# Last queries' stage of a decoder layer: attended chunks, reciprocals, stores and operand loads at other places, residual tiles in other buffers

## The chip, the cores and the metric

One Trainium2 chip, one of its NeuronCores. The metric is device time in microseconds (us) of one execution of the whole program; the time before is 2362.86 us, the median of 3 runs (2362.38 to 2368.84). Engines are called as the profile calls them: PE (TensorE matmul), PEld (its weight loads), DVE (VectorE), ACT (ScalarE), POOL (GpSimd), SP (SyncE, which here only issues DMAs).

## The reference

A pre-norm decoder layer on x of (2, 2048, 512), that is 4096 tokens, and a context of (2, 154, 512). In short:

```python
x = x + linear_attention(layernorm(x))        # 16 heads of 32, 128 features
x = x + cross_attention(layernorm(x), context)
x = x + experts(layernorm(x))                 # 8 experts, 6 picked, and a shared one
# linear_attention:
q_proj, k_proj = elu1(q @ proj), elu1(k @ proj)      # per head
kv, k_sum = k_proj^T v, sum(k_proj)                  # over all tokens of a batch
z = 1 / (q_proj . k_sum + 1e-8)
out = (q_proj kv * z) @ w_out + b_out
```

The layernorms have no weights. kv and k_sum are sums over all the keys of a batch, so no query of a batch can be finished before all its keys are done.

## The kernel before, in words

Tokens are cut into 8 blocks of 512 (`nblk`), 4 blocks to a batch (`bpb`); 512 columns are 4 chunks of 128 (`NC`), and a block is 4 tiles of 128 tokens (`NT`). Each fp32 matmul of a product is made of three fp32r matmuls on high and low parts (`TERMS`), so a 128x512 output of `product` takes 12 matmuls. One function writes the whole program, stage after stage:

1. Keys, values and queries of all blocks; on the way the queries of the first batch (blocks 0 to 3). Their numerators go to DRAM (`numd`). This ends near 493 us.
2. **The last queries' stage**, which the change touches: the queries of blocks 4 to 7, 16 chunks, one a step (`steps`, `for n in range(len(steps) + 1)`), from about 493 to 672 us. Beside them the attention output of blocks 0 to 5 is finished, and cross attention is begun.
3. Cross attention, with the attention output of blocks 6 and 7 at its start; then the experts.

What a step n of stage 2 does. `load_queries` (line 294 for its DMAs) loads the operand `qst` of a chunk, three DMAs of 256 KB. `query_features` makes four heads' features: a matmul `pqp` (L474), two activations (L359, L360) and a DVE instruction (L361, `e_q`). `numerators` and `denominators` of the chunk of the step before are 16 matmuls `pn` and `pd` (L230), then a copy `num` (L500). They are pinned: `tc.keep_in_program_order` ties each to the PE instruction written before it. After a block's fourth chunk `reciprocals` (L520) sends `den` to DRAM (`dd`, L523), reads it back spread out (`z`, L529), takes a DVE reciprocal (L532), pinned in the same way, and stores it (`zd`, L533).

Beside that runs the output of older blocks. `load_reciprocals` reads `zd` as `zr` (L546), `attended` multiplies `num` by it on POOL (L558), copies to a high part `at` on ACT (L559) and subtracts for a low part on DVE (L118). `load_numerators` brings `numd` of a block back by a DMA of 1 MB issued on POOL (L541). `attention_out` calls `out_tile` for each of a block's four tiles: load the residual tile `xr_a` (L306), add the bias row on POOL (L307), 12 matmuls `po_a` (L148), add on DVE (L310), store to `x1` (L311). `out_tile` also makes the output tiles of cross attention (`cross_out`).

What sets the order. Work that should fill gaps is a generator in `dense.waiting`; `dense.fill(k)` runs k of its matmuls at that place of the program, and `dense.after(k, f)` calls f when k such ticks have gone by. Program order is then only a priority: the context has `schedule_with_timeline_sim=True`, and when the program is built each engine's queue is put in the order in which the instructions are expected to become ready. On the chip each queue runs in that order and waits at its head. A tile's tag has a number of buffers, handed out in program order: a tile gets its buffer when its first writer goes, and a later tile of the tag does not go ahead of it. The tags that matter here:

- `b8` (17 buffers of 8 KB a partition): `qst`, the pairs `at`, `num` of a block, weights such as `xwq`, the layernorm's outputs, the cross attention's operands `xst`;
- `xs` (5 buffers): residual tiles `xr_a`, layernorm tiles `xsx`, raw weight tiles `xswout`, `xsxwq`;
- `hl` (4 buffers): the `zr` pairs, the high and low parts of queries on their way to DRAM;
- `eq` (5 buffers of the pool `early`): features of the first batch's queries. This pool is closed ahead of stage 2, and the pool `res`, with the four key tiles `xkst` of cross attention (`load_keys`, 12 DMAs issued on POOL, L631), takes its place in memory.

In the loop of stage 2, at the start of step n, `load_queries` is called for step n+1 and `attended` for two chunks (the table `ahead`: n to block and first chunk); in an even step the four output tiles of that block are added to `dense` and the next `load_numerators` follows. Then the four heads' features are written, in two halves with a `dense.fill` of 13 (later 14) after each, and after the second half the pinned numerators and denominators.

Of the kernel before, what the change touches and what calls it, by code (L numbers as in the profile page):

```python
# [9 lines left out]
F32 = mybir.dt.float32  # L10
# [7 lines left out]
P = 128  # L18
D = 512
# [5 lines left out]
NT = TB // P  # L25
# [12 lines left out]
def decoder_layer(  # L38
# [26 lines left out]
    nc = tc.nc  # L65
    tokens = x.shape[0]
    nblk = tokens // TB
    bpb = nblk // batches
# [4 lines left out]
    work = ctx.enter_context(tc.tile_pool(name="work", bufs=4))  # L73
# [8 lines left out]
    attending = ctx.enter_context(ExitStack())  # L82
    early = attending.enter_context(tc.tile_pool(name="early", bufs=5))
# [11 lines left out]
    def bank(name):  # L95
        return ps.tile([P, 512], F32, tag="ps", name=name)

    def eight(shape, dtype, name):
        return big.tile(shape, dtype, tag="b8", name=name)

    def half(name, dtype=F32):
        return work.tile([P, 512], dtype, tag="kp", name=name, bufs=9)
# [4 lines left out]
    def tile_of(d, b, t):  # L107
        at = b * TB + t * P
        return d[at : at + P, :]

    def load_row(d, name):
        row = rowp.tile([P, D], F32, tag="row", name=name)
        nc.sync.dma_start(out=row, in_=d.to_broadcast([P, D]))
        return row

    def low(dst, src, hi, eng=None):

        (eng or nc.vector).tensor_tensor(dst, src, hi.bitcast(F32), ALU.subtract)  # L118
# [7 lines left out]
    def split_weight(raw, name, busy=False):  # L126

        hi = eight([P, NC, D], FR, f"{name}_hi")
        lo = eight([P, NC, D], FR, f"{name}_lo")
        for k in range(NC):  # L130
            if isinstance(raw, list):
                part = raw[k]
            else:
                part = load_tile(raw, 0, k, name)
            if busy:
                nc.gpsimd.tensor_scalar(hi[:, k], part, 1.0, None, ALU.mult)
            else:
                nc.scalar.copy(hi[:, k], part)
            low(lo[:, k], part, hi[:, k], nc.gpsimd if busy or k % 2 else nc.vector)
        return hi, lo  # L140
# [3 lines left out]
    def product(dst, pairs):  # L144

        todo = [(a[i], b[j]) for a, b in pairs for i, j in TERMS]
        for n, (a, b) in enumerate(todo):
            nc.tensor.matmul(dst, lhsT=a, rhs=b, start=n == 0, stop=n == len(todo) - 1)  # L148
            yield
# [68 lines left out]
    dense = Dense()  # L218
# [16 lines left out]
    def fl(k, f):  # L235
        return int((k + 1) * f + 1e-6) - int(k * f + 1e-6)
# [55 lines left out]
    def stack(dst, d, parts=(0, 1, 0)):  # L292
        for r, part in enumerate(parts):
            nc.sync.dma_start(
                out=dst[r * HD : (r + 1) * HD].bitcast(F32),
                in_=d[part].rearrange("(h d) n -> d h n", d=HD),
            )
# [1 line left out]
    def store_pair(d, hl):  # L299
        nc.sync.dma_start(out=d.rearrange("r p n -> p r n"), in_=hl.bitcast(F32))  # L300

    def out_tile(name, src, dst, row, parts, w):


        xs = work.tile([P, D], F32, tag="xs", name=f"xr_{name}", bufs=5)
        nc.sync.dma_start(out=xs, in_=src)  # L306
        nc.gpsimd.tensor_tensor(xs, xs, row, ALU.add)  # L307
        po = bank(f"po_{name}")
        yield from product(po, [(part, (w[0][:, c, :], w[1][:, c, :])) for c, part in enumerate(parts)])
        nc.vector.tensor_tensor(xs, xs, po, ALU.add)  # L310
        nc.sync.dma_start(out=dst, in_=xs)  # L311

    x1 = [dram.tile([TB, D], F32, name=f"x1_{b}") for b in range(nblk)]
    x2 = [dram.tile([TB, D], F32, name=f"x2_{b}") for b in range(nblk)]
# [4 lines left out]
    xs = [half(f"xs{t}") for t in range(NT)]  # L319
# [8 lines left out]
    for t in range(NT):  # L328
# [4 lines left out]
        a = nc.scalar.copy(hi, pt)  # L333
        b = nc.vector.tensor_tensor(lo, pt, hi.bitcast(F32), ALU.subtract)
# [132 lines left out]
    def load_queries(b, c):  # L467
        qsts[b, c] = eight([3 * HD, 4, TB], FR, f"qst{b}_{c}")
        stack(qsts[b, c], qd[b][c])
# [47 lines left out]
    def reciprocals(b, pd):  # L517

        den = half(f"den{b}")
        nc.vector.tensor_scalar(den, pd, Z_EPS, None, ALU.add)  # L520
        dd = dram.tile([4, NC, TB], F32, name=f"dd{b}")
        for h in range(4):
            nc.sync.dma_start(out=dd[h], in_=den[h * HD : h * HD + NC, :])  # L523
        z = small.tile([P, H * TB // P], F32, tag="z", name=f"z{b}", bufs=1)
        flat = "h c n -> (h c n)"
        zd = dram.tile([4, NC, TB], F32, name=f"zd{b}")

        def turned():
            nc.sync.dma_start(out=z, in_=dd.rearrange(flat).rearrange("(p n) -> p n", p=P))  # L529

        def stored():
            tc.keep_in_program_order(nc.vector.reciprocal(z, z))  # L532
            nc.sync.dma_start(out=zd.rearrange(flat).rearrange("(p n) -> p n", p=P), in_=z)  # L533

        dense.after(10, turned)
        dense.after(18 if b < nblk - 1 else 24, stored)
        zds[b] = zd

    def load_numerators(b):
        nums[b] = eight([P, NC, TB], F32, f"num{b}")  # L540
        nc.gpsimd.dma_start(out=nums[b], in_=numd[b])  # L541

    def load_reciprocals(b, c):
        two = pair_of(f"zr{b}_{c}").bitcast(F32)
        for h in range(4):
            nc.sync.dma_start(  # L546
                out=two[h * HD : (h + 1) * HD],
                in_=zds[b][h : h + 1, c : c + 2].to_broadcast([HD, 2, TB]),
            )
        for i in range(2):  # L550
            zrs[b, c + i] = two[:, i]

    def attended(b, c):

        if c == 0:
            ats[b] = [eight([P, NC, TB], FR, f"at{b}_{i}") for i in range(2)]
        at = nums[b][:, c]
        nc.gpsimd.tensor_tensor(at, at, zrs.pop((b, c)), ALU.mult)  # L558
        nc.scalar.copy(ats[b][0][:, c], at)  # L559
        low(ats[b][1][:, c], at, ats[b][0][:, c])  # L560

    def attention_out(b, t):
        if not 0 <= b < nblk:
            return
        rows = slice(t * P, (t + 1) * P)
        hi, lo = ats[b]
        parts = [(hi[:, c, rows], lo[:, c, rows]) for c in range(NC)]
        yield from out_tile(f"a{b}_{t}", tile_of(x, b, t), tile_of(x1[b], 0, t), bout, parts, wout)


    scale = 1.0 / math.sqrt(HD)
# [187 lines left out]
    for s in range(ws_gate.shape[1] // F):  # L759
# [9 lines left out]
        out=before,  # L769
        in_=before,  # L770
# [498 lines left out]
    for n in range(nblk * per):  # L1269
        b, c, t = n // per, n // NT % NC, n % NT  # L1270
# [12 lines left out]
        if (b, c, t) == (nblk - 1, 3, 0):  # L1283
            load_numerators(0)
            load_reciprocals(0, 0)
            bout = load_row(b_out, "bout")
# [10 lines left out]
    for m in range((nblk - bpb) * per - shift, (nblk - bpb) * per + NT):  # L1297
# [3 lines left out]
            sums_step(m)  # L1301
        if m % 4 == 1:
            load_queries(*chunks[bpb * NC])
    attending.close()
    res = attending.enter_context(tc.tile_pool(name="res", bufs=1))


    wout = split_weight(w_out, "wout")
    steps = chunks[bpb * NC :]

    ahead = {n if n < 13 else n + 2: ((n - 1) // 2, (n - 1) % 2 * 2) for n in range(1, 15)}
    for n in range(len(steps) + 1):
        if n < len(steps):
            b, c = steps[n]
            if n + 1 < len(steps):
                load_queries(*steps[n + 1])
        for i in range(2):
            if n in ahead:
                attended(ahead[n][0], ahead[n][1] + i)
        if n + 1 in ahead:  # L1320
            load_reciprocals(*ahead[n + 1])
        if n in ahead and ahead[n][1]:
            whole = ahead[n][0]
            if whole < nblk - 2:
                dense.add(*(attention_out(whole, t) for t in range(NT)))
            if whole + 1 < bpb:
                load_numerators(whole + 1)
        if n == 7:
            ln, tr = layernorm(x1[0], 0, 0, qts, "x")
            dense.add(*ln[:3])  # L1330
            ln = ln[3:]
        if n == 8:
            dense.add(*tr[:1], *ln, *tr[1:])
        if n == 11:
            dense.add(*(cross_query(0, i) for i in range(NC)))
        for i in range(2):
            if n < len(steps):
                query_features(b, c, 2 * i)
                query_features(b, c, 2 * i + 1)
            dense.fill(fl(2 * n + i, 13 if n < 12 else 14))  # L1340
            if n and i:
                columns.batch()
                numerators(*steps[n - 1])
                denominators(*steps[n - 1])
        if n == 10:
            xwq = split_weight(wq_t, "xwq")
        if n == 11:
            for i in range(NC):
                load_keys(0, i)
    summed_up.close()  # L1350
# [2 lines left out]
    steps = [(b, c, t) for b in range(nblk) for c in range(NC) for t in range(NT)]  # L1353
    for n in range(len(steps) + LAG + 1):
        if n < len(steps):
            b, c, t = steps[n]
# [44 lines left out]
        if n > LAG:  # L1401
            b, c, t = steps[n - LAG - 1]
# [47 lines left out]
    for n, (group, u) in enumerate(todo3):  # L1450
# [3 lines left out]
        ahead = [[], []]  # L1454
        if u == len(units) - 2 and more:
            ahead = [expert_ahead(b) for b in range(group[-1] + 1, group[-1] + 3)]
        parts = products(n) if n else ready
# [123 lines left out]
```

## Time and profile before

| what | us |
|---|---|
| median of 3 runs | 2362.86 (2362.38 to 2368.84) |
| the profiled execution | 2363.39 |
| its span, first to last instruction | 2361.7 |
| PE busy | 2243.7 (95%) |
| DVE, POOL, ACT busy | 1670.7 (71%), 1218.7 (52%), 1105.2 (47%) |
| PE busy in 504 to 580, 76 us | 66.03, clock 0.94, DMA 234 GB/s |
| PE busy in 580 to 663, 83 us | 67.71, clock 0.90, DMA 215 GB/s |
| PE busy in 663 to 676, 13 us | 5.43, clock 0.67, DMA 164 GB/s |

The page's second part cuts the span into 40 slices of 59 us; a digit is the busy share in tenths, and PEclk is the clock that TensorE was granted. In a list by time, a row is start, length, engine, line, operation, output<-input and count; in brackets stands how long the engine was idle before it and what it waited for. In the list of waits, a row is who waited for whom, us in total, times, and the longest.

### The profile page before, as it was taken

The page shows a single profiled execution, that of the slowest core. Times are in us where ns is not written, and L with a number is a line of the kernel's source. Part 1 is how long each engine was busy: PE and PEld are TensorE (multiplying, and loading weights), DVE is VectorE, ACT ScalarE, POOL GpSimd, SP SyncE. Part 2 cuts the span into 40 slices and gives each one's busy share as a digit, 9 for nine tenths or more (in the row PEclk, how much of TensorE's full clock was granted, in tenths as well). Part 3 has the DMA queues.
Part 4 walks back from the last instruction along what each step waited for, and adds up shares of the span by engine and source line. Part 5 has one row for each costly group of instructions (what it writes and reads, how often), then busy time and mean ns, then how long its engine had stood idle before and what let it go on. Part 6 is the DMA issues. An engine that isn't in the chain of part 4 may idle for free.

```text
span 2361.7 us, 35144 instructions
## 1 busy us (share of the span) xinstructions
PE 2243.7 (95%) x11978; PEld 1735.2 (73%) x11978; DVE 1670.7 (71%) x2777; ACT 1105.2 (47%) x2598; POOL 1218.7 (52%) x1086
## 2 busy tenths in 40 slices
PE   7999999897878999998999999999999999999999
PEld 5888777654556777776778877888778888788887
DVE  6555564666567777778877786677887778977777
ACT  4555676754556667776433343322333222432221
POOL 5545333645356565554655553545555455754543
PEclk9999999998989999999999999999999999999999
DMA  6655777997765566564766654655547555575553
GB/s 207 181 171 169 208 214 218 253 254 214 224 189 174 159 188 171 169 193 174 263 240 240 227 192 186 243 199 227 193 170 277 205 205 218 210 260 198 223 187 129
DMA packets 194896, 485.63 MB, mean 206 GB/s; under 512 B 26970, under 2 KB 46810, under 8 KB 174782
## 3 DMA queue, kind: packets, MB, share of 16 engines
q1 hardware_dynamic: 192990, 477.30, 61.3%
q0 software_dynamic: 1728, 6.09, 0.9%
q8 instruction: 95, 1.56, 0.3%
q14 instruction: 83, 0.68, 0.1%
HBM read 345.01 MB, written 138.31 MB: 205 GB/s over the span
## 4 chain that ended last, share of the span: by engine, by line
PE 51%; DMA 7%; DVE 7%; POOL 3%; issue 2%; ACT 1%; SPq 0%; DVEq 0%; ACTq 0%; POOLq 0%
PE pg L1045 26%; PE pf L1158 10%; PE pf L148 3%; PE po_x L148 3%; PE xpq L148 2%; PE pc L737 2%; PE xpt L717 1%; PE psc L685 1%; DMA xr_x<-x 1%; DMA wq<-wqs 1%; DMA xqd<-xhl 1%; DMA xsx<-x 1%; DMA xst<-xqd 1%; DMA x<-xr_x 1%; DVE nb L692 1%
## 5 line engine op out<-in xcount | busy, mean ns | idle before, releaser
L1045 PE MATMUL pg<-xo,wq 128*128 128x512 f32 x3360 | 826.1, 394 | 8.5 <-DMA wq<-wqs 3.5
L1045 PEld LDWEIGHTS pg<-xo,wq 128*128 128x128 f32 x3360 | 631.6, 189 | 151.0 <-ACT s L1056 5.8
L1179 DVE TENSOR_TENSOR sum<-sum,pf 128x512 f32<-128x512 f32 x376 | 251.2, 683 | 57.2 <-PE pf L1158 49.8
L402 POOL TENSOR_TENSOR kacc<-kacc,e_k 128x512 f32<-128x512 f32 x128 | 166.3, 1300 | 215.3 <-DVE e_k L361 208.6
L695 ACT ACTIVATE xe<-psc,nb 128x154 f32<-128x154 f32 x512 | 194.7, 403 | 62.3 <-DVE nb L692 52.3
L700 POOL TENSOR_TENSOR xe<-xe,sm 128x616 f32<-128x616 f32 x128 | 156.8, 1232 | 105.8 <-DVE sm L699 74.9
L1108 POOL TENSOR_TENSOR u<-u,gr 128x512 f32<-128x512 f32 x48 | 62.6, 1304 | 273.5 <-DVE u L1077 258.3
L1158 PE MATMUL pf<-ht,wdo 128*128 128x512 f32 x696 | 186.4, 393 | 1.0 <-DVE sum L1179 1.0
L361 DVE SCALAR_TENSOR_TENSOR e_k<-pp,e_k 128x512 f32<-128x512 f32 x128 | 87.5, 685 | 106.4 <-ACT e_k L360 93.0
L1158 PE MATMUL pf<-hb,wdo 128*128 128x512 f32 x522 | 147.8, 399 | 5.9 <-DVE sum L1179 5.9
L1158 PEld LDWEIGHTS pf<-ht,wdo 128*128 128x128 f32 x696 | 129.8, 188 | 30.6 <-DVE sum L1179 1.7
L1076 ACT ACTIVATE u<-u 128x512 f32<-128x512 f32 x80 | 50.6, 632 | 206.6 <-DVE u L1065 203.9
L148 PE MATMUL pf<-wd,hp 128*128 128x512 f32 x528 | 133.2, 399 | 3.7 <-DVE acc L1238 2.2
L692 DVE TENSOR_REDUCE nb<-psc 128x2 f32<-128x308 f32 x256 | 111.5, 468 | 27.3 <-PE psc L685 26.6
L148 PEld LDWEIGHTS pf<-wd,hp 128*128 128x128 f32 x528 | 99.3, 189 | 29.9 <-issue 3.6
L1158 PEld LDWEIGHTS pf<-hb,wdo 128*128 128x128 f32 x522 | 97.4, 189 | 30.4 <-DVE sum L1179 7.6
L1065 DVE TENSOR_TENSOR u<-u,pg 128x512 f32<-128x512 f32 x160 | 108.1, 681 | 8.7 <-PE pg L1045 7.9
L695 ACT ACTIVATION_READ_ACCUMULATOR xe<-psc,nb 128x1 f32 x512 | 110.9, 217 | 0.0
L359 ACT ACTIVATE e_k<-pp 128x512 f32<-128x512 f32 x128 | 76.8, 601 | 68.4 <-PE pp L397 62.8
L685 PE MATMUL psc<-xkst,xst 96*128 96x154 f32 x512 | 88.4, 282 | 12.3 <-DVE e_q L361 7.6
L685 PEld LDWEIGHTS psc<-xkst,xst 96*128 96x128 f32 x512 | 75.7, 192 | 32.0 <-ACT xe L695 11.5
L397 PEld LDWEIGHTS pp<-pst,kst 96*128 96x128 f32 x512 | 75.9, 192 | 28.3 <-issue 8.8
(280 smaller groups left out, 5129.7 us busy)
## 6 DMA issues: line engine op xcount, KB each, us to landing
wq<-wqs SPq DMA_DIRECT2D x90, 1024.0 KB
wqs<-wq SPq DMA_DIRECT2D x30, 1024.0 KB
wdo<-wds SPq DMA_DIRECT2D x29, 1024.0 KB
kst<-kd SPq DMA_DIRECT2D x96, 256.0 KB
qst<-qd SPq DMA_DIRECT2D x96, 256.0 KB
xst<-xqd SPq DMA_DIRECT2D x96, 256.0 KB
wdo<-wds SPq DMA_DIRECT2D x29, 768.0 KB
kd<-khl SPq DMA_DIRECT2D x32, 512.0 KB
```

The costliest lines, as they stand in the source:

```text
L148: nc.tensor.matmul(dst, lhsT=a, rhs=b, start=n == 0, stop=n == len(todo) - 1)
L359: nc.scalar.activation(e, src, AF.Relu, scale=-1.0)
L361: nc.vector.scalar_tensor_tensor(e, src, 0.0, e, ALU.max, ALU.add)
L402: nc.gpsimd.tensor_tensor(acc, acc, kp, ALU.add)
L685: nc.tensor.matmul(psc[:, i], lhsT=xsts[b, c][:, h, t * P : (t + 1) * P], rhs=ksts[bt, c][:, h, :], start=True, stop=True,)
L692: nc.vector.tensor_reduce(nb[:, two], psc, AX.X, ALU.max, negate=True)
L695: nc.scalar.activation(e[:, h, :], psc[:, i], AF.Exp, bias=nb[:, h : h + 1], accum_out=sm[:, h : h + 1],)
L700: nc.gpsimd.tensor_tensor(e, e, sm.unsqueeze(2).to_broadcast([P, 4, keys]), ALU.mult)
L1045: nc.tensor.matmul(pb, lhsT=w[:, p, i, k, :], rhs=xop[:, q, k, :], start=first and m == 0, stop=m == len(todo) - 1, skip_group_check=True,)
L1065: nc.vector.tensor_tensor(dst, dst, pb, ALU.add)
L1158: nc.tensor.matmul(banks[i], lhsT=w[:, p, i * P : (i + 1) * P], rhs=t[q], start=new and m == 0, stop=m == len(TERMS) - 1, skip_group_check ...
L1179: nc.vector.tensor_tensor(dst, dst, banks[i], ALU.add)
```

## The change

The pool `early` stays open until step 11. Until then residual tiles go to its tag `eq` in place of `xs`, and each `attention_out` tile loads the residual of the next tile when it starts. The pool `res` and `load_keys` come after that. The store of an output tile is called 8 ticks later, and a block's reciprocal and its store 26 ticks after the denominators in place of 18 (the last block stays at 24). Query operands are called two steps ahead. `attended` is called for one chunk after each half's fill, and a block's output tiles and the next `load_numerators` follow the second one. The diff:

```diff
-    def out_tile(name, src, dst, row, parts, w):
-
-
-        xs = work.tile([P, D], F32, tag="xs", name=f"xr_{name}", bufs=5)
+    open_early = [True]
+
+    rests = {}
+
+    def load_rest(name, src):
+        if open_early:
+            xs = early.tile([P, D], F32, tag="eq", name=f"xr_{name}")
+        else:
+            xs = work.tile([P, D], F32, tag="xs", name=f"xr_{name}", bufs=5)
         nc.sync.dma_start(out=xs, in_=src)
+        rests[name] = xs
+
+    def out_tile(name, src, dst, row, parts, w, ahead=None):
+
+
+        if name not in rests:
+            load_rest(name, src)
+        xs = rests.pop(name)
+        if ahead and open_early:
+            load_rest(*ahead)
         nc.gpsimd.tensor_tensor(xs, xs, row, ALU.add)
...
         nc.vector.tensor_tensor(xs, xs, po, ALU.add)
-        nc.sync.dma_start(out=dst, in_=xs)
+        dense.after(8, lambda: nc.sync.dma_start(out=dst, in_=xs))
...
-        dense.after(18 if b < nblk - 1 else 24, stored)
+        dense.after(26 if b < nblk - 1 else 24, stored)
...
-        yield from out_tile(f"a{b}_{t}", tile_of(x, b, t), tile_of(x1[b], 0, t), bout, parts, wout)
+        ahead = (f"a{b}_{t + 1}", tile_of(x, b, t + 1)) if t < NT - 1 else None
+        yield from out_tile(
+            f"a{b}_{t}", tile_of(x, b, t), tile_of(x1[b], 0, t), bout, parts, wout, ahead
+        )
+
+    def attention_outs(b):
+        return [attention_out(b, t) for t in range(NT)]
...
-    attending.close()
-    res = attending.enter_context(tc.tile_pool(name="res", bufs=1))
...
     for n in range(len(steps) + 1):
         if n < len(steps):
             b, c = steps[n]
-            if n + 1 < len(steps):
-                load_queries(*steps[n + 1])
-        for i in range(2):
-            if n in ahead:
-                attended(ahead[n][0], ahead[n][1] + i)
+            for at in range(1 if n == 0 else n + 2, min(n + 3, len(steps))):
+                load_queries(*steps[at])
         if n + 1 in ahead:
             load_reciprocals(*ahead[n + 1])
-        if n in ahead and ahead[n][1]:
-            whole = ahead[n][0]
-            if whole < nblk - 2:
-                dense.add(*(attention_out(whole, t) for t in range(NT)))
-            if whole + 1 < bpb:
-                load_numerators(whole + 1)
...
             dense.fill(fl(2 * n + i, 13 if n < 12 else 14))
+            if n in ahead:
+                attended(ahead[n][0], ahead[n][1] + i)
+                if ahead[n][1] and i:
+                    whole = ahead[n][0]
+                    if whole < nblk - 2:
+                        dense.add(*attention_outs(whole))
+                    if whole + 1 < bpb:
+                        load_numerators(whole + 1)
             if n and i:
                 columns.batch()
                 numerators(*steps[n - 1])
...
         if n == 11:
+            open_early.clear()
+            attending.close()
+            res = attending.enter_context(tc.tile_pool(name="res", bufs=1))
             for i in range(NC):
                 load_keys(0, i)
```

## Prediction

> **What bounds the kernel now.** I read the page's second part first, for where PE is not full.
>
> ```profile
> PE   7999999897878999998999999999999999999999
> ...
> PEclk9999999998989999999999999999999999999999
> DMA  6655777997765566564766654655547555575553
> ```
>
> Slices ten to thirteen (531 to 767 us) read 7, 8, 7, 8, and only ten and twelve have a lower PEclk. Behind them PE reads 9 but for one 8, so what stage 2 loses comes back nowhere, and what it saves is saved. Next come the waits of PE from 480 to 740 us, and then PE's list by time, for each hole.
>
> ```profile
> PE pqp L474 <- DMA qst<-qd: 11.2, 3, 5.3
> PE psc L685 <- DVE e_q L361: 7.6, 1, 7.6
> PE pn L230 <- DVE xr_a L310: 6.4, 3, 3.7
> PE pqp L474 <- DVE xsx L252: 4.1, 1, 4.1
> ```
>
> ```profile
> 554.47 1.04 PE L230 MATMUL pd<-e_q,ksz 128*32 128x512 f32 x8
> 560.82 0.77 PE L474 MATMUL pqp<-qst,pst 96*128 96x512 f32 x1 [5.31 <-DMA qst<-qd]
> ...
> 563.95 1.05 PE L148 MATMUL po_a<-wout_hi,at 128*128 128x512 f32 x2
> 564.80 0.48 PE L148 MATMUL po_a<-wout_lo,at 128*128 128x512 f32 x1
> 565.12 0.62 PE L148 MATMUL po_a<-wout_hi,at 128*128 128x512 f32 x2
> ```
>
> See two losses in the second list: the hole, and behind it matmuls at half speed (a pair in 1.05 us, later in 0.62). From 560.82 to 565.12 ten matmuls took 4.3 us where 0.23 each is usual: 2.0 us lost. Worked out likewise, the holes are, with what follows them cold:
>
> - A, query operands late: 1.19 (at 530.7), 5.31 + 2.0 (at 555.5), 4.65 + 1.6 (at 652.6): 14.75.
> - B, the layernorm's fourth tile late (at 596.4): 4.12 + 2.4 = 6.5.
> - C, at 539.8 to 545.4: 2.15 + 0.62 + 0.71 = 3.5; DVE had stood 7.97 us before an `at`.
> - D, at 580.3: 3.71 + 2.3 = 6.0; again DVE stood behind an `at` that waited for `zr`.
> - E, at 629.7: 1.7; DVE stood 6.06 us for a layernorm tile of the next stage.
> - F, at 664.1: 7.57 + 2.6 = 10.2, where steps 15 and 16 have no filler.
> - G, at 447.3: 3.9; the pinned reciprocal held DVE 6.21 us.
>
> Together 46.5 us. But DMA is a second bound: from 504 to 580 us it moved 234 GB/s x 76 us = 17.8 MB, and from 580 to 663, 215 x 83 = 17.8 MB. The best 10 us slices of the stage run at 259 to 271 GB/s; at 265 either half takes 67 us. So at most 9 us can go in the first half and 16 in the second.
>
> **The change part by part.**
>
> *Query operands a step earlier.* Nothing is added: 48 DMAs at about 0.4 us on SP are placed elsewhere. Why are they late? SP's list shows it.
>
> ```profile
> 648.34 0.47 SPq L294 DMA_DIRECT2D xst<-xqd  x1
> 648.85 0.93 SPq L294 DMA_DIRECT2D qst<-qd  x1
> 649.88 0.79 SPq L533 DMA_DIRECT2D zd<-z  x1
> 650.72 0.97 SPq L294 DMA_DIRECT2D qst<-qd  x2
> ```
>
> The last chunk's operand goes right behind the cross operand `xst`, which waits for its own round trip through DRAM. Tag b8 gives buffers in program order; before, that `qst` was written after three `xst` and after block 7's `num`. Called a step earlier it stands ahead of all of them, behind block 5's `at` (608 us): some 30 us sooner. The chunk that left the 5.31 us hole stood behind block 5's `num` (first written at 548.0) and moves ahead of it, and of block 2's `at` (540.2), to behind the load of block 2's numerators (519.5): again some 20 us. A2 and A3 should go. What is late next there is DMA bandwidth, hence the caps.
>
> *Residual tiles in eq, a tile ahead; keys after step 11.* In `xs` the fourth layernorm tile stood behind block 3's four residual tiles; alone in `xs` with the weights it can load with the other three (553.9 to 565.5 us). B goes. The 20 residual tiles of blocks 0 to 4 keep their 20 loads of 0.35 us; five that went at 451 to 472 us, among a DMA share of 1.0, now wait for the features to leave `eq`, at 485 to 493 us. POOL stood 40.9 us, 9 times, for residual tiles in the stage, and `at` behind it, so C should shrink. The 12 key DMAs cost POOL 12 x 0.55 = 6.6 us; before they ran at 494.6 to 502.1, when POOL had nothing else, now after the last `eq` tile is stored, about step 13, when POOL has only block 5's residuals; the keys have 4.1 us to land and are first read after step 16. Between nothing and 6.6 us I take 2, since POOL was idle from 632.4 to 663.7 us; queued behind them would be the residual adds, and behind those DVE and a PSUM bank.
>
> *Attended chunks after the fills, outputs a step later.* The same 32 POOL multiplies (1.29 us), copies (0.62) and subtractions (1.12). Features now have the priority over them on ACT and DVE, and `zr` gets half a step (5 us) more to land, against C and D. Counting ticks, block 0's outputs start in step 3, not 2, block 5's end in step 16, not 15. Step 1, which has no outputs, took from 499.8 to 505.3 us, 5.5 us with 2.8 us of warm matmul work; a second such step adds 2.7 us idle and some cold clock, and takes as much from the empty steps at the end (F). I charge 3 and credit F with half; the bounds are none of it and all.
>
> *Reciprocal 8 ticks later.* Eight ticks are 2 us of PE or more. Before, DVE stood 6.21, 2.82 and 7.31 us for `z` (at 444, 501, 641). I credit G with half, 2; the other two stood beside full PE or in F. If `zr` is late for it, that shows in block 6 only, read at step 15.
>
> *Store 8 ticks later.* Taken at nothing: `xkst`, written in step 11, ran at 494.6, so queues follow readiness more than place, and a store is ready when its add is done. Its cover is that `x1` is read several steps later. At worst it frees `eq` 2 us later, a tile.
>
> **The sum.** First half: A1, A2, C are 12.0, cap 9, taken 7. Second: A3 and B are 12.8, D and E 7.7, cap 16, taken 13. F 5.1, G 2.0. Gains 27.1. Against: the empty step 3, keys 2, and new holes: 27.2 us of DVE waits for `at`, 8 of 3.4 us, stay in the stage, two of them now show as C and D, and behind closed holes two more should show: 7. Net 27.1 - 12 = 15.1, and 2363.39 - 15.1 = 2348.3; the median lies 0.5 under the profiled run, so 2348.
>
> On the cold stretches: here the five holes of 3.7 us and more were followed by 3.4 to 5.7 us at half speed, those of 1.2 to 2.2 us by none. The Trainium skill (TensorE: Matmul & The Clock Gate, Part 1) has the clock halved after an idle window of about 3.4 us and back after as long a busy one; the trace agrees. By that rule F, cut to half (3.8 us), would keep its whole cold stretch, and the estimate would be 1.3 us higher.
>
> **The rivals.**
>
> *DMA takes it back.* Loads moved forward displace others on a full DMA (share 0.89 to 0.96 at 520 to 540 and 560 to 580 us). For it: A's first two holes lie behind 2.5 MB each (six operand DMAs and the numerators), issued within 4 and 7 us. Against: 540 to 550 stands at 0.54, 580 to 590 at 0.32. Then A, C, D stay, and B, half of F and G (13.6) meet the costs of 12: 2361. Chance 0.20.
>
> *Slower: b8 runs full.* With a third operand alive, step 10 counts: `pst` 1, `wout` 2, `num` of blocks 4 to 6, `at` of blocks 3 and 4 (4), layernorm 2, operands 3, `xwq` 2: 17 of 17. From one more on, that is if block 3's outputs, which end in step 10, run late, block 5's `at` waits and everything behind it in the tag. Price: a chain of two multiplies, copies and subtractions (2.6 + 1.2 + 2.2 = 6) with 2.3 cold, in step 11 and again when the `xst` come, 16.6 in all; with the costs of 12, against B, F and G (13.6), 2363.4 + 15 = 2378. Chance 0.16.
>
> *All holes close.* 9 + 16 + 10.2 + 3.9 - 5 = 34: 2329. Chance 0.12.
>
> *The calls don't move the queues.* As for the store; for operands and residual tiles it would need the buffer order to be of no account, which the two lists speak against. It falls in with the first rival.
>
> **The numbers.** The forecast (2337 to 2356) has 0.52. A measurement of this kernel tells from no change what exceeds 0.3%, 7 us. Faster: 0.52 + 0.12 = 0.64; same: 0.20; slower: 0.16. Leaving out the slower rival and a little of the best, the range is 2328 to 2370.
>
> **What would show it.** Right: no wait of `pqp` for `qst` over 1 us; `qst` of the last chunk issued before 630 us; the fourth `xsx` next to the third; no DVE wait of 6 us for `z`; key DMAs on POOL near 640; the first `psc` some 15 us sooner. Wrong: PE holes of the same size under other names, above all `at`, or DMA at 1.0 throughout.

## The result, and the profile after

| | before | after |
|---|---|---|
| median, 4 runs each on the same chip, us | 2362.62 (2360.81 to 2368.84) | 2344.42 (2341.92 to 2348.36) |
| profiled execution, and its span | 2363.39, 2361.7 | 2341.92, 2340.1 |
| PE busy in the span | 2243.7 (95%) | 2240.0 (96%) |
| waits of PE of 1.5 us or more, 493 to 680 us, summed from its list by time | 29.2, 7 times | 7.8, twice |

The change is faster: ratio 0.992, 95% interval 0.9896 to 0.9944, 18.2 us. 2348 was forecast, 15 us less than before. The three rows of the page's second part that the prediction began with read, for the changed kernel:

```profile
PE   7999999989989999999999999999999999999999
...
PEclk9999999999999999999999999999999999999999
DMA  6555777999964566565665546555457556575553
```

The four poor slices of PE, ten to thirteen (7, 8, 7, 8 before), now read 9, 9, 8, 9, and PEclk reads 9 in all. DMA reads 9 in slices ten and eleven (526 to 643 us), where it read 7. The waits of PE from 480 to 740 us begin:

```profile
PE pqp L489 <- DVE e_q L376: 10.6, 6, 4.8
PE psc L706 <- ACT xe L716: 2.4, 6, 0.6
PE xpv L148 <- DVE num L512: 2.3, 1, 2.3
```

Before, this list began with 11.2 us for `qst`, 7.6 for `e_q` at the first scores (`psc`), 6.4 for `xr_a` at `pn` and 4.1 for `xsx` at `pqp`. Of the four, 0.6 us for `e_q` at `psc` is left. What is left is DVE: the longest wait of the stage is a new one, at 590 us, and the rows around it tell its chain (start, length, engine, line, output<-input; in brackets the idle time before):

```profile
578.97 0.55 DVE L547 RECIPROCAL z<-z 128x64 f32<-128x64 f32 x1 [4.26 <-DMA z<-dd]
...
584.89 1.71 SPq L561 DMA_DIRECT2D zr<-zd  x4
...
591.22 2.49 POOL L573 TENSOR_TENSOR num<-num,zr 128x512 f32<-128x512 f32 x2 [7.51 <-DMA zr<-zd]
...
593.17 1.09 DVE L118 TENSOR_TENSOR at<-num,at 128x512 fp32r<-128x512 f32 x1 [7.68 <-ACT at L574]
...
594.91 0.80 PE L489 MATMUL pqp<-qst,pst 96*128 96x512 f32 x1 [4.76 <-DVE e_q L376]
```

The reciprocal of block 5 is done at 579.5, the loads of its `zr` are issued from 584.9 on, POOL stands 7.51 us for them, DVE stands 7.68 us behind POOL at the head of its queue with the next `e_q` behind that, and PE stands 4.76 us.

**Where the time went.** Both traces hold the same 11978 matmuls, in part in another order. The time at which the same number of them has started, before less after, is the lead of the changed kernel. It is 2.8 us at 100 us of the kernel before and 3.1 at 303, where no instruction of the change has run yet (a difference between two executions), 3.3 at 463, 13.5 at 578, 34.6 at 678, 23.9 at 718, 22.4 at 771, 22.6 at 1668 and 21.6 at 2321. So 18.5 us are the change's, and some 11 us of the 34.6 are lost again between 678 and 718. The table of engines by stretch (length, then PE, PEld, DVE, ACT, POOL busy with instructions, the clock granted, DMA share, GB/s) tells why; the stretches are cut so that PE has the same number of matmuls in both, within two, before first:

```profile
463.00:578.00 115.00, 100.41 (x518) 60.37 (x519) 73.64 (x117) 61.14 (x114) 60.22 (x58) 0.91 0.90 251
578.00:678.00 100.00, 77.15 (x361) 46.34 (x360) 59.83 (x95) 45.21 (x92) 39.35 (x36) 0.86 0.72 203
678.00:718.00 40.00, 38.07 (x228) 31.25 (x227) 30.89 (x64) 28.07 (x111) 31.99 (x25) 1.00 0.62 192
718.00:900.00 182.00, 170.64 (x1130) 128.25 (x1129) 135.88 (x314) 125.67 (x520) 105.70 (x115) 1.00 0.59 171
```

and after:

```profile
459.70:564.50 104.80, 93.53 (x519) 53.91 (x520) 77.94 (x123) 62.67 (x118) 56.01 (x50) 0.97 0.96 268
564.50:643.40 78.90, 72.34 (x362) 46.32 (x361) 51.02 (x74) 41.17 (x76) 39.63 (x37) 0.96 0.89 244
643.40:694.10 50.70, 41.81 (x229) 32.95 (x227) 39.84 (x79) 32.05 (x132) 35.45 (x33) 0.97 0.61 182
694.10:877.30 183.20, 173.14 (x1128) 130.17 (x1130) 134.46 (x313) 124.42 (x515) 105.08 (x115) 0.98 0.59 169
```

The first two stretches became 31.3 us shorter, the third 10.7 longer. See the counts of the other engines: in the second stretch DVE has 21 instructions fewer and ACT 16 fewer than before, in the third 15 and 21 more, and POOL 8 more. The changed kernel runs some of their work later, and PE, idle for 1.9 us of the third stretch before, is idle for 8.9 us there now. So part of the lead at 678 us was borrowed. Over all four, 437.0 us became 417.6, 19.4 less. PE's idle time went from 50.7 to 36.8, which is 13.9, and its busy time from 386.3 to 380.8, which is 5.5: the same matmuls at a higher granted clock (0.91 and 0.86 in the first two stretches before, 0.97 and 0.96 after).

### The profile page after: what moved, and what is told of

Its sections match the earlier page's. It is cut to its first block, busy times and chain, and to the rows that moved or that the text cites. A ratio compares the mean times of both kernels' runs of the same rounds, so it can differ in the third digit from the quotient of the medians.

```text
span 2340.1 us, 35134 instructions
## 1 busy us (share of the span) xinstructions
PE 2240.0 (96%) x11978; PEld 1732.0 (74%) x11978; DVE 1680.5 (72%) x2777; ACT 1105.1 (47%) x2598; POOL 1220.8 (52%) x1086
## 4 chain that ended last, share of the span: by engine, by line
PE 49%; DVE 9%; DMA 6%; POOL 4%; issue 3%; ACT 2%; SPq 1%; DVEq 0%; ACTq 0%; POOLq 0%
PE pg L1066 24%; PE pf L1179 10%; PE xpq L148 3%; PE po_x L148 3%; PE pf L148 2%; PE pc L758 2%; PE xpt L738 2%; PE psc L706 1%; DMA xr_x<-x 1%; DMA rgu<-in_w_up 1%; DVE u L1098 1%; DVE u L1086 1%; POOL hp L118 1%; DVE wq L118 1%; DMA wq<-wqs 1%
## 5 line engine op out<-in xcount | busy, mean ns | idle before, releaser
L1179 PEld LDWEIGHTS pf<-hb,wdo 128*128 128x128 f32 x522 | 97.4, 189 | 30.4 <-DVE sum L1200 7.7
```

The lines of the kernel that those rows point to most:

```text
L1179: nc.tensor.matmul(banks[i], lhsT=w[:, p, i * P : (i + 1) * P], rhs=t[q], start=new and m == 0, stop=m == len(TERMS) - 1, skip_group_check ...
```

## The experiments

Twelve kernels in three groups, each beside runs of the kernel before on the same chip (medians 2370.1, 2364.3 and 2362.05 us; e1 to e4, e5 to e8, e9 to e12). The ratio is the one on record and not the quotient of the two medians, which is 0.9923 for e2, 0.9932 for e3 and 0.9921 for e4; a difference of 0.001 is not to be relied on. "Residual part" stands for tiles in `eq`, loaded a tile ahead, with the keys after step 11. The last three columns are from each profile: DMA's rate in 504 to 580 us, POOL's waits for residual tiles in 493 to 680 us, and the waits of PE of 1.5 us or more there.

| kernel | median | ratio to before, 95% | GB/s | POOL | PE |
|---|---|---|---|---|---|
| before (the profile shown) | 2362.62 | 1 | 234 | 37.7 | 29.2 |
| the change | 2344.42 | 0.992, 0.9896 to 0.9944 | 265 | 16.5 | 7.8 |
| e1 operands alone | 2368.60 | 0.9996, 0.9982 to 1.0011 | 240 | 28.9 | 30.4 |
| e2 residual part alone | 2351.82 | 0.9909, 0.9889 to 0.9929 | 261 | 14.4 | 16.2 |
| e3 chunks alone | 2353.92 | 0.9924, 0.9907 to 0.9942 | 222 | 37.3 | 20.8 |
| e4 change, reciprocal at 18 | 2351.41 | 0.9913, 0.9894 to 0.9932 | 267 | 14.4 | 10.9 |
| e5 the change again | 2347.69 | 0.9922, 0.9902 to 0.9942 | 265 | 12.8 | 7.8 |
| e6 change without residual part | 2359.95 | 0.9981, 0.9967 to 0.9994 | 233 | 23.4 | 21.2 |
| e7 change without chunks | 2351.17 | 0.9936, 0.9916 to 0.9957 | 265 | 13.6 | 19.5 |
| e8 change, operands one step ahead | 2351.49 | 0.9942, 0.992 to 0.9963 | 267 | 9.2 | 14.0 |
| e9 residual part without the tile ahead | 2346.47 | 0.9929, 0.9914 to 0.9944 | 259 | 13.1 | 19.5 |
| e10 before without POOL's bias add | 2355.28 | 0.9969, 0.9957 to 0.998 | 239 | no add | 21.4 |
| e11 residual part and chunks | 2346.48 | 0.993, 0.9918 to 0.9942 | 268 | 19.7 | 16.8 |
| e12 change, stores at once | 2338.87 | 0.9905, 0.989 to 0.992 | 268 | 8.4 | 9.4 |

**The parts one by one.** e1 puts only the operands into the kernel before:

```diff
-            if n + 1 < len(steps):
-                load_queries(*steps[n + 1])
+            for at in range(1 if n == 0 else n + 2, min(n + 3, len(steps))):
+                load_queries(*steps[at])
```

> The kernel before with query operands called two steps ahead, and nothing else of the change. The theory on record: the holes of 5.31 and 4.65 us in which pqp waits for qst go, with their cold stretches, 13.5 us in all, of which the room of DMA in the first half leaves some 10: 2350 to 2355 us. Rival, DMA takes it back: the waits return under other names, 2360 us or more. A second rival, the parts only work together: operands come sooner, and the next wait (the attended chunks behind zr and residual tiles) fills the same holes: 2358 us or more, with no pqp wait for qst over 1 us.

It is no change: 0.9996. The waits of PE, 480 to 740 us, show that the operands did what they should, and that it bought nothing:

```profile
PE psc L685 <- DVE e_q L361: 11.2, 3, 5.7
PE pn L230 <- DVE xr_a L310: 10.5, 4, 5.5
PE pqp L474 <- DVE e_q L361: 9.5, 6, 3.6
```

`qst`, 11.2 us before, is not in the list at all. The same time stands under `xr_a` and `e_q`, both DVE. Where the hole of 5.31 us was (560.8), the trace of e1 has this:

```profile
562.44 5.40 POOL L558 TENSOR_TENSOR num<-num,zr 128x512 f32<-128x512 f32 x4 [8.66 <-DMA num<-numd]
...
563.74 0.62 ACT L559 CAST at<-num 128x512 fp32r<-128x512 f32 x1 [7.41 <-POOL num L558]
...
564.39 1.09 DVE L118 TENSOR_TENSOR at<-num,at 128x512 fp32r<-128x512 f32 x1 [7.24 <-ACT at L559]
...
566.13 0.79 PE L474 MATMUL pqp<-qst,pst 96*128 96x512 f32 x1 [3.61 <-DVE e_q L361]
```

The operand is there, and the features are not made, since DVE stands 7.24 us before an `at` whose numerators come by a load issued on POOL at 551.9. Earlier POOL had stood 11.68 us for a residual tile. The kernel before has the same rows beside its hole of 5.31 us, which ends at 560.82:

```profile
560.53 6.01 POOL L558 TENSOR_TENSOR num<-num,zr 128x512 f32<-128x512 f32 x4 [10.05 <-DMA num<-numd]
...
562.48 1.12 DVE L118 TENSOR_TENSOR at<-num,at 128x512 fp32r<-128x512 f32 x1 [7.05 <-ACT at L559]
```

So DVE stood there until 562.48, longer than PE stood for the operand. Was it bandwidth? No:

```profile
504.00:580.00 76.00, 66.02 (x307) 41.38 (x299) 47.39 (x74) 40.68 (x76) 33.30 (x31) 0.91 0.89 240
580.00:663.00 83.00, 70.75 (x335) 42.36 (x333) 47.67 (x72) 36.53 (x69) 27.64 (x24) 0.92 0.74 206
```

DMA moved 240 and 206 GB/s, below the 261 and 233 of the next kernel in the same windows.

e2 is the residual part alone: `load_rest`, `ahead`, `early` kept open, and the keys after step 11, as in the diff above.

> The kernel before with residual tiles of blocks 0 to 4 in eq, a tile ahead, the pool kept open to step 11 and the keys loaded behind it; operands, attended chunks, reciprocal and stores as before. The theory on record: the layernorm's fourth tile loads with the other three, its hole of 4.1 us with 2.4 cold goes, and some of the 3.5 us around 540; less 2 for the key DMAs: 2354 to 2358 us. Rival: tag xs was no limit, and the keys on POOL cost more than it brings: 2362 us or more.

```profile
PE pqp L489 <- DMA qst<-qd: 7.2, 2, 5.2
PE psc L703 <- DVE e_q L376: 6.8, 1, 6.8
```

It is 0.9909, as much as the whole change and more than its forecast (2354 to 2358 us are 0.996 to 0.998 of 2362.86). In its list by time no wait of PE over 1.5 us from 493 us on ends before 583 us; the operand hole of 560.8 went too, though operands are called as before. Four of 1.5 us or more stay: 2.25 at 584.0, 1.92 for `qst` at 596.1, the last chunk's (5.25 at 647.0) and F (6.78 at 660.8).

e3 moves `attended`, the outputs and `load_numerators` behind the fills, in the kernel before.

> The kernel before with attended chunks after each half's fill and outputs and numerators after the second, that is outputs a step later. The theory on record: half of the 10.2 us at the stage's end and half of the 6.0 at 580 come in, 3 us for a second step without outputs go out: 2355 to 2360 us. Rival: operands and residual tiles still arrive as late as before, so the moved chunks meet the same holes and the empty step is a pure loss: 2363 to 2367 us.

0.9924, again more than forecast (0.997 to 0.999), with DMA at only 222 GB/s in the first half and POOL's waits for residual tiles unchanged (37.3 us). So there are two separate ways to nearly the same gain, and by the ratios the parts don't add: their sum would be 1.67%. e4 is the change with the old place of the reciprocal:

```diff
-        dense.after(26 if b < nblk - 1 else 24, stored)
+        dense.after(18 if b < nblk - 1 else 24, stored)
```

> The changed kernel with the reciprocal at 18 ticks, as before. The theory on record gives the 8 ticks 2 us: 2346 to 2347 us against 2344.4, and DVE waits for z of 4 to 7 us are back. Rival, from the trace of the changed kernel: the zr of block 5 arrives late there (POOL waits 7.5 us for it at 584 to 591, and a hole of 4.76 us follows on PE at 590), since its reciprocal is made later; without the 8 ticks that hole goes and the time is 2339 to 2342 us.

0.9913: the ticks can't be told from nothing. The sign given for them did not come either: DVE waits for `z` for 8.0 us in 493 to 680 us, 3.3 the longest, with 18 ticks, and for 7.8 us, 4.3 the longest, with 26. A hole of 3.83 us at 600 us, behind a wait of POOL of 7.63 us for `zr`, is in e4 too, so the later reciprocal did not make the new hole of the change.

**The change without a part.** e5 repeats the change, e6 to e8 undo one part each.

> The changed kernel once more, to stand on the same chip as the next three. Both theories: 0.990 to 0.994 of the time before.

> The change without its residual part: residual tiles in xs again, keys early; operands, chunks, stores and reciprocal as changed. Each part alone gave 0.9909 (residual), 0.9924 (chunks), 0.9996 (operands). Theory S, substitutes: POOL, which runs in order, stands for residual tiles and takes the attended chunks, DVE and PE with it; residual tiles in eq and attended chunks moved behind the fills each break that chain, so either is enough: 0.990 to 0.995 here. Theory on record, parts that add: without the residual part its 0.9% is gone again, 0.999 to 1.002.

> The change with attended chunks, outputs and numerators at the start of the step, as before; operands, residual tiles, stores and reciprocal as changed. Theory S: residual tiles alone break the chain, and operands now come in time as well, so 0.988 to 0.992, no worse than the whole change. Parts that add: the chunks' 0.76% is gone again, 0.998 to 1.001.

> The change with query operands called one step ahead, as before. If operands matter once the chain on POOL is broken, as the forecast's term for them would then still hold in part, the hole of 4.65 us with 1.6 cold in front of the last chunk's features is back: 0.994 to 0.997. If they are of no account even then: 0.990 to 0.993 and no wait of pqp for qst over 2 us.

Against e5, only e6 is apart: 12.3 us slower (2359.95 against 2347.69), and the intervals don't meet. Without the chunks 3.5 us are lost, without the operands 3.8, each with overlapping intervals. e6 speaks against theory S as it was put: 0.9981 is outside its 0.990 to 0.995, so here the moved chunks did not stand in for the residual part, and it is below the 0.999 to 1.002 of parts that add, by less. POOL stood as long there as before: 23.4 us for residual tiles and, by the trace, 12.1 more at the same add for a store. e7 (0.9936) lies between the ranges of the two theories. e8 (0.9942) lies in the range where the operands count, but without its sign: `pqp` waits for `qst` for 2.5 us in all, 1.3 the longest, so that too stays open. e11 is e2 and e3 together:

> The residual part and the moved chunks together; operands, stores and reciprocal as before. Each alone gave 0.9909 and 0.9924. Theory S, substitutes: 0.988 to 0.993. Parts that add: 0.983 to 0.986.

0.993, no better than either alone. Its lead over before, counted by matmuls, is 32.9 us at 678 us and 15.0 at 690; e9, which has no moved chunks, has 14.9 and 15.1. The moved chunks bring PE to the stage's end sooner and leave work of other engines for the cross attention, as in the table by stretch. That the parts do not add rests on the medians: in single traces the lead won from 303 to 771 us is 8.0 in e2, 6.2 in e3 and 13.4 in e11, which nearly adds. All three are set against a trace of another group, and the first two are from the group whose kernel before was the slowest, so the traces don't decide it.

**What in the residual part does it.** e9 takes the call a tile ahead out of e2, so that only the buffers and the keys' place are left:

```diff
-        if ahead and open_early:
-            load_rest(*ahead)
```

> The kernel before with residual tiles of blocks 0 to 4 in eq and the keys after step 11, but each tile's load called when the tile starts, not a tile ahead. If the free buffers are the cause, as queues follow buffers and readiness more than place: 0.989 to 0.993 of the time before, as the whole residual part alone (0.9909), and POOL waits for residual tiles of 10 to 20 us from 493 to 680 us (37.7 before, 14.4 with the whole part). If calling a tile ahead is the cause: 0.996 or more, with POOL waits near 30 us.

0.9929, not to be told from e2: the buffers, with the keys later, are enough. The two go together, since the pool of the keys takes the place of `early` in memory, and no run moves the keys alone. In the kernel before their last load had landed at 504.6 us, as the first half began, so they do not fill DMA there; that their place has no other part in the gain is not shown. e10 tests whether it is POOL, standing in its queue before the bias add, that costs, by taking the add away:

```diff
-        nc.gpsimd.tensor_tensor(xs, xs, row, ALU.add)
+        if name[0] != "a":
+            nc.gpsimd.tensor_tensor(xs, xs, row, ALU.add)
```

> The kernel before without the POOL add of the bias row in attention output tiles: b_out is left out of the sum there, 32 POOL instructions of 1.3 us. Residual tiles stay in xs and arrive as before, but POOL no longer stands for them ahead of the attended chunks. Theory S, the cause is POOL's in-order wait for residual tiles: 0.989 to 0.994, the DVE waits for at go from 25.9 to 10 to 15 us. Rival, the cause is the shared tag xs (late layernorm tile, SP standing for stores) wherever the wait falls: 0.997 or more, DVE now stands for the residual tiles itself.

The waits of DVE, 493 to 680 us, in e10:

```profile
DVE z L533 <- DMA z<-dd: 19.0, 3, 8.4
DVE st_x L245 <- DMA xsx<-x: 12.3, 4, 6.8
DVE xr_a L311 <- PE po_a L148: 12.1, 4, 6.3
DVE at L118 <- ACT at L560: 7.1, 5, 3.2
```

The wait for `at` fell from 25.9 to 7.1 us, further than that theory had it, and the time by 0.31% only, a shade under the rival's 0.997; that is some third of what e2 gains, and 8.8 us slower than e9 in the same group. The rival's sign did not come: DVE stands for residual tiles themselves for 2.0 us only. It stands for `z` and `xsx`, and PE for `qst` (6.1 at 595.1, 3.1 at 651.3). So POOL's wait ahead of the bias add can be part of it and is not the whole.

**The stores.** e12 is the change with the store where it was:

```diff
-        dense.after(8, lambda: nc.sync.dma_start(out=dst, in_=xs))
+        nc.sync.dma_start(out=dst, in_=xs)
```

> The changed kernel with each output tile's store called at once, not 8 ticks later. The theory on record takes the 8 ticks at nothing: 0.991 to 0.994, as the change. Rival, it frees the buffers of xs and eq sooner: 0.988 to 0.990; or SP stands longer for DVE (20.2 us for stores in the changed kernel): 0.995 or more.

0.9905, the lowest of all and between the first two ranges, with an interval that overlaps those of the change (0.992 and 0.9922). Later stores bring nothing that can be measured; that they cost something is not shown.

## Why the prediction was right in the total and wrong in its parts

| term | forecast, us | measured in the two traces, lead by matmuls |
|---|---|---|
| reciprocal later (G) | 2.0 | 0.2 (3.1 at 303, 3.3 at 463) |
| first half, A1, A2, C | 7, cap 9 | 10.2 (13.5 at 578) |
| second half with F, less costs of 12 | 13 + 5.1 - 12 = 6.1 | 21.1 (34.6 at 678) |
| behind the stage | 0 | -13.0 (21.6 at 2321) |
| sum | 15.1 | 18.5 |

*The step that failed* is the operands': "A2 and A3 should go. What is late next there is DMA bandwidth, hence the caps". They go, the last chunk's `qst` is issued at 598.2 to 599.4 us in the changed kernel (the list of SP), and alone they leave the time as it was: e1. Late next was DVE, standing in its queue before an `at`, behind POOL, behind a load; at 240 and 206 GB/s DMA had room. I had read each hole as the property of the transfer that ended last in it. The chain beside it had its own lateness of about the same size (7.05 us on DVE against 5.31 on PE, in the trace I had), and the residual part shortens it: e2's trace has none of A2, B, C and D, and one new hole of 2.25 us near D; I had credited it B and a share of C. I had named `at` as what shows next, and charged 7 us for the whole change; for the operands alone the charge was their whole credit.

*Parts that add.* The sum was made as if each part took its own holes. Alone the residual part gives 0.91%, the chunks 0.76%, both 0.70%, all 0.8%. That the total came out is in part luck: the operands' credit was too large and the residual part's too small, and in the table the second half is some 15 us above its forecast and the stretch behind the stage 13 below.

*The caps on DMA* hold as a size: I took 265 GB/s, and kernels with the residual part reach 259 to 268 in the first half, those without 222 to 240. But 9 us as the most for the first half did not hold: of the 10.2 us, 10.0 were won between 504 and 578.

*The residual part.* B is gone: block 0's four `xsx` are loaded from 527.3 to 535.0 us (before 553.9 to 591.7, the fourth last). POOL's waits for residual tiles fell from 37.7 to 16.5 us. The keys run on POOL at 611.5 to 618.2, not near 640 as the sign had it, after POOL had stood 5.64 us for the store of an output tile; no wait of PE names them, and of the 2 us charged nothing is seen.

*Chunks after the fills.* F, forecast at half, is gone whole: the first `psc` starts at 638.4 us, 25 us sooner, not 15. What paid for it is the stretch that I thought fixed: "what stage 2 loses comes back nowhere, and what it saves is saved" does not hold, since the matmuls that took 40.0 us behind 678 before take 50.7 now. And hole D was misread: DVE stood only 0.84 us before that `at`, and was then busy with two subtractions (2.77 us) and an add until PE went on.

*Reciprocal and G.* The hole G stayed, 3.94 us in both traces, and so did the wait of DVE for `z` ahead of it, 6.21 us in both. From 303 to 463 us the lead grew by -0.1 to 2.1 us in the six traces with 26 ticks and by -2.8 to 0.2 in the seven others with 18, one execution each: a hint, no more. In the stage DVE's waits for `z` fell from 11.6 to 7.8 us, 4.3 the longest, so the sign "no wait of 6 us" came there, though not at G; it is in e4 with 18 ticks too, so the ticks did not bring it. G had also been entered without a cold stretch; in the trace the clock is 0.50 from about 452.3 to 455.7 us.

*Store.* Taken at nothing, and nothing was measured (e12).

*Cold stretches.* The new hole of 4.76 us is followed by pairs at 1.05 us where 0.62 is usual, as after the holes of before. 5.5 of the 19.4 us in the table by stretch are busy time of the same matmuls; pricing a hole with its stretch was right.

*The rivals.* That DMA takes it back describes what became of the operands (e1, 0.9996), but by another cause. Tag `b8` running full did not come: the longest wait for an `at` in the change (7.68 us) stood behind `zr`, which is not of that tag, and the kernel is faster. The forecast's sign that would have shown it wrong, "holes of the same size under other names, above all `at`", is what e1 shows, and what the 4.76 us hole of the change shows once.

**What stays open.** Why the residual part gives three times what e10 gives is not settled. The kernels with it are the ones with a DMA rate of 259 GB/s and more in the first half; that is a mark of them, and whether it is cause or effect no run tells. SP standing for a store to land before it loads a residual or a layernorm tile into the same buffer is another such mark, a narrow one: 26.2 us in before and 27.8 to 32.9 in the others without the residual part, 14.5 to 24.8 in those with it. Nor is it shown why the change without the residual part (0.9981) is worse than the chunks alone (0.9924), which were measured in another group; up to 771 us e6's trace is not behind (a lead of 10.4 us against 6.3), it falls behind later (5.3 against 7.6 at 2321).

## What to carry to other kernels

A hole that ends with a transfer is not that transfer's until the chain beside it has been followed: ask when the next instruction of every in-order engine could have run, and credit only the difference. Try the parts of a change alone before their gains are added, because holes in one stage can be substitutes; here buffers of their own for one kind of load (with the keys later) gave as much as everything together, as far as the medians tell. And follow the lead past the end of the stage, with the counts of all engines by stretch, for a lead can be work put off.

## What the runs showed of the hardware that I had not expected

A hole shorter than I had thought needed turned the clock down. In the changed kernel PE stood 3.07 us before 496.24; the granted clock was 0.79 in 496.2 to 498.2, 0.50 in 498.2 to 500.2 and 0.90 up to 503.0; in slices of 0.5 us it falls to 0.50 between 497.0 and 497.5, about 1 us after the hole had ended. The Trainium skill (TensorE: Matmul & The Clock Gate, Part 1) has the halving follow an idle window of about 3.4 us, with a free-running window. The 3.07 us are under its length, and it is no single case: in e10 a hole of 2.07 us before 530.70 was followed by a clock of 0.50 to about 534, while 2.15 us before 541.90 in the kernel before were followed by none. So a hole of 2 us can be enough in these traces, and the measurement decides against 3.4 us of idle as a condition.

DMA held 265 to 268 GB/s for 76 us on end in six kernels (e4, e5, e7, e8, e11, e12) and in the change, where I had seen 259 to 271 only in slices of 10 us.

And the subtraction for the low part on DVE (`at`), which I had priced at 1.12 us, takes 0.66 to 0.70 us alone: so in all 69 rows of the 14 traces with no POOL instruction beside it. In 320 of the 342 rows that began with a POOL instruction under way (0.15 us or more of it left), it ended 0.53 to 0.57 us after that instruction had, and took up to 1.84 us. In the chain at 590 us it began at 593.17, POOL's multiply ended at 593.71 and it ended at 594.26. So the 1.09 us are in part a wait for POOL that a list by time shows as DVE's busy time.
